# The first load moved ahead of the weight matrices on the loading queue

## The chip, the cores and the metric

The kernel runs on one core of a Trainium2 chip. The metric is the time of one execution in device microseconds; three runs of the kernel before took 325.69 to 325.96 us, median 325.85. A core has a matrix engine (TensorE, PE in the profile), a vector engine (VectorE, DVE), ScalarE (ACT), GpSimd (POOL) and SyncE (SP), each with a queue of its own, and 16 DMA engines that all of them share. Here ScalarE and SyncE compute nothing: ScalarE issues loads, SyncE issues stores.

## The reference

```python
# x: (128, 128, 1024) float32, itok_B_0_7: (128,) int32 in 0..7, L0_cond_weights: (8, 128, 128) float32
w = weights[subjects]                        # one 128 x 128 matrix for each of 128 samples
out = jnp.einsum('bct,bcd->bdt', x, w)       # B, C, D, T = 128, 128, 128, 1024
return x + out
```

Each sample is a matrix of 128 channels by 1024 times (512 KB). It is multiplied by the matrix of its subject, one of eight, and added to the product.

## The kernel before

The 128 samples are taken in 32 turns of four (`NT` = 32, index `i`), and each turn in two pairs (`j`, 64 pairs in all). Twelve buffers of four samples (`xs`, `SLOTS` = 12) hold what is loaded; a result is written back over its input, and stored from there. So a buffer goes from load to product, to addition, to store, and is loaded again twelve turns later.

All work is written out by hand, with semaphores. What each queue does, in its order:

- **ScalarE** issues the load of the eight weight matrices into `w_all` (line 161; 512 KB in 1024 pieces of 512 B, one row of one matrix each), and then the 128 loads of the samples (line 169, through `load` and `transfer`, where the profile has them as line 57). Each takes 512 KB in 32 pieces of 16 KB: the samples' rows are spread so that four rows of 4 KB lie together in memory. Until turn 12 nothing holds these loads back but the queue. From turn 12 on, ScalarE waits until the buffer has been stored (lines 164 to 167).
- **SyncE** issues the load of the 128 subject numbers (`given`, line 141), and then the stores (lines 221 to 223): two of 1 MB in turn 0, one of 2 MB in each turn from 1 to 30, and three pieces in turn 31.
- **VectorE** writes zeros (line 143), makes the subject numbers safe as indices (lines 153 to 157), and then adds product and input for one pair at a time (line 217).
- **GpSimd** reads indices into registers, 16 at a time (line 185), waits once for `w_all` (line 193), and copies the matrix of each sample out of `w_all` into one of four buffers (line 196). From the third pair on, the first copy of a pair also waits for the pair's loads, and for the addition two pairs ago.
- **TensorE** starts with three matmuls on zeros (line 146), waits for the loads of the first two pairs itself (line 181), and for the copies of a pair (line 203); then it multiplies, in pieces of 512 columns (line 206).

The two samples of a pair share one semaphore (`s_pair`), so a pair is free to go when both its samples have landed. At the end ScalarE waits for the last stores (lines 227 to 230).

What sets the order around the change is ScalarE's queue: its transfers go to the same 16 DMA engines one after the other, and in the trace the first packets of sample 0 start where the last ones of the matrices end. The stores come from another queue and mix with the loads.

Of the kernel before, what the change touches and what calls it, by code (L numbers as in the profile page):

```python
# [41 lines left out]
DMA = 16  # L42
# [7 lines left out]
def transfer(nc, engine, out, in_):  # L50

    later, nc._always_lower_symbolic_ap = nc._always_lower_symbolic_ap, False
    ins, outs = engine.lower_ap_dma(in_), engine.lower_ap_dma(out)
    nc._always_lower_symbolic_ap = later
    return engine.add_instruction(  # L57
        mybir.InstDMACopy(
            name=nc.get_next_instruction_name(),
            engine=engine.engine,  # L60
            ins=ins,
            outs=outs,
            mode="Copy",
            cce_op=ALU.bypass,
            queue=QUEUES[engine.engine],
        )
    )


@with_exitstack  # L70
def kernel(
    ctx: ExitStack,
    tc: tile.TileContext,
    x: bass.AP,
    subjects: bass.AP,
    weights: bass.AP,
    out: bass.AP,
):
    nc = tc.nc
    B, C, T = x.shape  # L80
    S, _, D = weights.shape
    NT = B // (G * H)

    def sbuf(name, *shape, dtype=F32):
        return ctx.enter_context(nc.sbuf_tensor(name, list(shape), dtype)).ap()

    given, near, wrap, index = (
        sbuf(name, 1, B, dtype=I32) for name in ("given", "near", "wrap", "index")
    )
    w_all = sbuf("w_all", C, S, D)  # L90
    ws = [sbuf(f"w{i}", C, 1, D) for i in range(W_SLOTS)]
    zeros = sbuf("zeros", C, N)
    xs = [sbuf(f"x{i}", C, H * G, T) for i in range(SLOTS)]
    ps = [
        ctx.enter_context(nc.psum_tensor(f"ps{i}", [D, G, T], F32)).ap() for i in range(P_SLOTS)
    ]

    s_given = tc.alloc_semaphore("s_given")
    s_wall = tc.alloc_semaphore("s_wall")
    s_index = tc.alloc_semaphore("s_index")  # L100
    s_zeros = tc.alloc_semaphore("s_zeros")
    s_copied = tc.alloc_semaphore("s_copied")
    s_product = tc.alloc_semaphore("s_product")
    s_added = tc.alloc_semaphore("s_added")

    s_pair = [[tc.alloc_semaphore(f"s_pair{i}_{h}") for h in range(H)] for i in range(SLOTS)]


    s_first = tc.alloc_semaphore("s_first")

    def emptied(i, h):

        turns = i // SLOTS
        return (DMA * G + (DMA if h == H - 1 else 0)) * turns

    def loaded(i, q):

        h = q // G
        return s_pair[i % SLOTS][h], emptied(i, h) + DMA * G

    def load(engine, i, q):
        k, h = i % SLOTS, q // G
        transfer(
            nc,
            engine,
            xs[k][:, q, :],
            x[i * H * G + q].rearrange("(a r) t -> a (r t)", r=ROWS),
        ).then_inc(s_pair[k][h], DMA)

    def store(i, q0, q1):  # L130
        k, b = i % SLOTS, i * H * G
        transfer(
            nc,
            nc.sync,
            out[b + q0 : b + q1].rearrange("g d t -> d g t"),
            xs[k][:, q0:q1, :].rearrange("d (o g) t -> d o (g t)", g=min(G, q1 - q0)),
        ).then_inc(s_first if i == 0 and q1 == G else s_pair[k][(q1 - 1) // G], DMA)

    with tc.tile_critical():  # L139

        nc.sync.dma_start(given, subjects.rearrange("(o b) -> o b", o=1)).then_inc(s_given, DMA)

        nc.vector.memset(zeros, 0.0).then_inc(s_zeros, 1)  # L143
        nc.tensor.wait_ge(s_zeros, 1)
        for _ in range(IDLE):
            nc.tensor.matmul(  # L146
                ps[P_SLOTS - 1][:, G - 1, :N], zeros[:, :D], zeros, start=True, stop=True
            )

        nc.vector.wait_ge(s_given, DMA)
        nc.vector.tensor_scalar(near, given, -S, S - 1, ALU.max, ALU.min).then_inc(s_index, 1)  # L153
        nc.vector.wait_ge(s_index, 1)
        nc.vector.tensor_scalar(wrap, near, 0, S, ALU.is_lt, ALU.mult).then_inc(s_index, 1)  # L155
        nc.vector.wait_ge(s_index, 2)
        nc.vector.tensor_tensor(index, near, wrap, ALU.add).then_inc(s_index, 1)  # L157
        nc.gpsimd.wait_ge(s_index, 3)


        nc.scalar.dma_start(w_all, weights.rearrange("s c d -> c s d")).then_inc(s_wall, DMA)  # L161
        for i in range(NT):
            k = i % SLOTS
            if i == SLOTS:
                nc.scalar.wait_ge(s_first, DMA)
            if i >= SLOTS:
                nc.scalar.wait_ge(s_pair[k][H - 1], emptied(i, H - 1))
            for q in range(H * G):
                load(nc.scalar, i, q)


        for j in range(NT * H):
            i, q0, q1 = j // H, j % H * G, (j % H + 1) * G
            k = i % SLOTS
            p = ps[j % P_SLOTS]

            ahead = j < P_SLOTS
            if ahead:  # L180
                nc.tensor.wait_ge(*loaded(i, q0))
            for q in range(q0, q1):
                b = i * H * G + q
                if b % R == 0:
                    _, subject = nc.values_load_multi_w_load_instructions(
                        index[0:1, b : b + R],
                        engines=[mybir.EngineType.Pool],
                        min_val=0,
                        max_val=S - 1,
                        skip_runtime_bounds_check_because="the index is clamped on the chip above",  # L190
                    )
                if b == 0:
                    nc.gpsimd.wait_ge(s_wall, DMA)
                if not ahead and q == q0:
                    nc.gpsimd.wait_ge(s_added, j - P_SLOTS + 1)
                copy = nc.gpsimd.tensor_copy(  # L196
                    ws[b % W_SLOTS], w_all[:, bass.ds(subject[b % R], 1), :]
                )
                if not ahead and q == q0:
                    copy.wait_op(*loaded(i, q0), "sem-ge")  # L200
            copy.then_inc(s_copied, 1)

            nc.tensor.wait_ge(s_copied, j + 1)
            for q in range(q0, q1):
                for t in range(0, T, N):
                    mm = nc.tensor.matmul(  # L206
                        p[:, q % G, t : t + N],
                        ws[(i * H * G + q) % W_SLOTS][:, 0, :],
                        xs[k][:, q, t : t + N],
                        start=True,  # L210
                        stop=True,
                    )
            mm.then_inc(s_product, 1)

            mine = xs[k][:, q0:q1, :]
            nc.vector.wait_ge(s_product, j + 1)
            nc.vector.tensor_tensor(  # L217
                mine, p, mine, ALU.add
            ).then_inc(s_added, 1)

            if i == 0 or q1 == H * G or i == NT - 1:
                nc.sync.wait_ge(s_added, j + 1)
                store(i, q0 if i in (0, NT - 1) else 0, q1 - (b == B - 1))

    with tc.tile_critical() as waits:
        for i in range(NT - SLOTS, NT):
            nc.scalar.wait_ge(s_pair[i % SLOTS][H - 1], emptied(i + SLOTS, H - 1))
        nc.scalar.wait_ge(s_pair[(NT - 1) % SLOTS][0], emptied(NT - 1 + SLOTS, 0) + DMA)  # L230
    last = nc.sync.dma_start(out[B - 1], xs[(NT - 1) % SLOTS][:, H * G - 1, :])

    tc.add_manual_dep(
        last.ins,
        waits.name,
        mybir.DependencyInfo(mybir.DependencyClass.NoSync, mybir.DependencyReason.SCHED_ONLY),
        reason="the end of the program waits for it",
    )
# [27 lines left out]
```

## Time and profile before

| | |
|---|---|
| median of three runs | 325.85 us (325.69 to 325.96) |
| the profiled execution | 326.15 us |
| its span, first to last instruction | 324.4 us |
| moved by DMA | 134.85 MB, 416 GB/s over the span |
| PE busy | 240.2 us (74%) |
| DVE busy | 147.9 us (46%) |
| POOL busy | 34.3 us (11%) |
| `w_all`, issue to landing | 4.3 us |
| a load of x, issue to landing (median) | 32.2 us |
| a store of 2 MB, issue to landing (median) | 46.9 us |

The profile is that of one execution. Its page divides the span into 40 slices of 8.1 us and gives for each the busy tenths of an engine and the rate of the DMA. Other views give a table for any stretch of time, the instructions in order of time, and, for a DMA, when it was issued and when it landed; the trace also has a record of each DMA packet, with its start, length, size and queue. The issue of a DMA is shown on the queue of its engine (ACTq, SPq); it is not counted as busy time, and the transfer itself starts later. A window counts a packet where it starts, so a share can be over 1 in a short stretch. The time of an execution is 1.77 us longer than the span in this profile; that part lies around the span.

### The profile page before, as it was taken

To read this page: it belongs to the slowest core of one execution; us is meant where nothing else is said; L and a number is where in the kernel's file an instruction comes from. 1 tells how busy PE (TensorE), PEld (TensorE's weight loads), DVE (VectorE), ACT (ScalarE), POOL (GpSimd) and SP (SyncE) were. 2 spreads that over 40 slices of the span, in tenths; PEclk is the share of its full clock that TensorE was granted. 3 is DMA by queue.
4 is the path that set the end of the run, shared out by engine and by line. 5 is a ranking of instruction groups with operands and counts; after the bars stand their busy time and mean duration, and the time that the engine had idled before them with its cause. 6 is when DMAs were issued, how large, how long until landed. Compare 5 with 4: busy or idle time off the path is not lost.

```text
span 324.4 us, 1608 instructions
## 1 busy us (share of the span) xinstructions
PE 240.2 (74%) x518; PEld 94.5 (29%) x518; DVE 147.9 (46%) x68; POOL 34.3 (11%) x132
## 2 busy tenths in 40 slices
PE   7999987888888888888988888888888768000000
PEld 2444432333333333333333333333333323000000
DVE  1475754555555555555555555554554553200000
POOL 1011110111111111111011111111111010000000
PEclk9999999999999999999999999999999999855555
DMA  7999999999999999999999999999999999999995
GB/s 263 402 418 426 426 421 425 425 425 423 428 425 422 427 418 427 427 424 424 428 423 421 423 427 426 419 429 426 423 426 427 417 435 417 425 427 424 429 426 243
DMA packets 16074, 134.85 MB, mean 416 GB/s; under 512 B 2625, under 2 KB 3650, under 8 KB 3906
## 3 DMA queue, kind: packets, MB, share of 16 engines
q10 hardware_dynamic: 7184, 67.64, 49.8%
q1 hardware_dynamic: 8882, 67.11, 49.3%
q8 instruction: 4, 0.07, 0.1%
q14 instruction: 4, 0.03, 0.0%
HBM read 67.63 MB, written 67.11 MB: 415 GB/s over the span
## 4 chain that ended last, share of the span: by engine, by line
PE 41%; DVE 20%; issue 18%; POOL 4%; DMA 2%; POOLq 1%; ACTq 0%; SPq 0%
PE ps L206 41%; DVE x L217 20%; POOL w L196 4%; DMA x<-in_x_dram 2%; POOLq L196 1%; ACTq L57 0%; ACTq L161 0%; ACTq L262 0%; SPq L139 0%
## 5 line engine op out<-in xcount | busy, mean ns | idle before, releaser
L206 PE MATMUL ps<-x,w 128*128 128x512 f32 x512 | 234.7, 604 | 33.6 <-POOL w L196 32.9
L217 DVE TENSOR_TENSOR x<-ps,x 128x2048 f32<-128x2048 f32 x64 | 146.7, 2292 | 128.1 <-PE ps L206 128.1
L206 PEld LDWEIGHTS ps<-x,w 128*128 128x128 f32 x512 | 92.6, 189 | 176.5 <-issue 92.3
L196 POOL COPY w<-w_all 128x128 f32 x128 | 34.1, 296 | 237.2 <-DMA x<-in_x_dram 207.2
L146 PE MATMUL ps<-zeros 128*128 128x512 f32 x6 | 5.5, 1088 | 1.7 <-DVE zeros L143 1.7
L146 PEld LDWEIGHTS ps<-zeros 128*128 128x128 f32 x6 | 1.8, 328 | 3.7 <-issue 2.1
L143 DVE MEMSET zeros<- 128x512 f32 x1 | 0.5, 485 | 1.1 <-SPq L139 1.1
L153 DVE TENSOR_SCALAR near<-given 1x128 int32<-1x128 int32 x1 | 0.2, 216 | 0.6 <-DMA given<-in_itok_B_dram 0.6
L157 DVE CUSTOM_DVE_ANT_0 index<-near,wrap 1x256 uint16<-1x256 uint16 x1 | 0.3, 278 | 0.0
L155 DVE TENSOR_SCALAR wrap<-near 1x128 int32<-1x128 int32 x1 | 0.2, 215 | 0.0
L253 POOL MEMSET const-float32-0.0<- 128x1 f32 x1 | 0.1, 99 | 0.2 <-issue 0.2
L253 POOL MEMSET const-bfloat16-1.0<- 128x1 bf16 x1 | 0.1, 102 | 0.0
L253 POOL MEMSET const-uint8-127<- 128x1 uint8 x1 | 0.1, 102 | 0.0
L253 POOL MEMSET const-float32-1.0<- 128x1 f32 x1 | 0.1, 99 | 0.0
## 6 DMA issues: line engine op xcount, KB each, us to landing
x<-in_x_dram ACTq DMA_DIRECT2D x128, 512.0 KB, 32.2
out_dram<-x SPq DMA_DIRECT2D x30, 2048.0 KB, 46.9
out_dram<-x SPq DMA_DIRECT2D x3, 1024.0 KB, 13.8
out_dram<-x SPq DMA_DIRECT2D x2, 512.0 KB, 21.0
w_all<-in_L_cond_weights_dram ACTq DMA_DIRECT2D x1, 512.0 KB, 4.3
given<-in_itok_B_dram SPq DMA_DIRECT2D x1, 0.5 KB
```

The source lines that it names most:

```text
L143: nc.vector.memset(zeros, 0.0).then_inc(s_zeros, 1)
L146: nc.tensor.matmul(ps[P_SLOTS - 1][:, G - 1, :N], zeros[:, :D], zeros, start=True, stop=True)
L153: nc.vector.tensor_scalar(near, given, -S, S - 1, ALU.max, ALU.min).then_inc(s_index, 1)
L155: nc.vector.tensor_scalar(wrap, near, 0, S, ALU.is_lt, ALU.mult).then_inc(s_index, 1)
L157: nc.vector.tensor_tensor(index, near, wrap, ALU.add).then_inc(s_index, 1)
L196: copy = nc.gpsimd.tensor_copy(ws[b % W_SLOTS], w_all[:, bass.ds(subject[b % R], 1), :])
L206: mm = nc.tensor.matmul(p[:, q % G, t : t + N], ws[(i * H * G + q) % W_SLOTS][:, 0, :], xs[k][:, q, t : t + N], start=True, stop=True,)
L217: nc.vector.tensor_tensor(mine, p, mine, ALU.add).then_inc(s_added, 1)
L253: nc = _bacc.Bacc("TRN2", target_bir_lowering=False, num_devices=1)
```

## The change

The load of the matrices is taken from its place ahead of the loop, and issued inside the loop behind the load of sample 0. The other 127 loads stay behind both. Nothing else is moved, and no wait is added or removed.

```diff
-        nc.scalar.dma_start(w_all, weights.rearrange("s c d -> c s d")).then_inc(s_wall, DMA)
         for i in range(NT):
             k = i % SLOTS
             if i == SLOTS:
...
             for q in range(H * G):
                 load(nc.scalar, i, q)
+                if i == 0 and q == 0:
+                    nc.scalar.dma_start(w_all, weights.rearrange("s c d -> c s d")).then_inc(s_wall, DMA)
```

## The prediction

> **What bounds the kernel now.** I read the 40 slices first, because the kernel moves 134.85 MB and computes little, then the DMA share stretch by stretch at both ends of the run, then the order of time around the first load. From the page:
>
> ```profile
> PE   7999987888888888888988888888888768000000
> DVE  1475754555555555555555555554554553200000
> ...
> DMA  7999999999999999999999999999999999999995
> GB/s 263 402 418 426 426 421 425 425 425 423 428 425 422 427 418 427 427 424 424 428 423 421 423 427 426 419 429 426 423 426 427 417 435 417 425 427 424 429 426 243
> ```
>
> The transfers are busy from the first slice to the last, at about 425 GB/s, while PE has nothing left for the last six slices. TensorE is high in the middle, but a data transfer ends the run 40 us after the last matmul. So the chain of waits, which gives 41% to PE, isn't the bound: a later matmul only means a later store in a queue that is full anyway. The time is: the moment the DMA engines start, plus the time their packets take, plus the gaps between packets, plus the uneven end. Windows over both ends (columns: stretch and length, busy time and count of PE, PEld, DVE, POOL, granted clock, DMA share, GB/s):
>
> ```profile
> 1.50:2.00 0.50, 0.32 (x1) 0.33 (x2) 0.12 (x1) 0.00 (x0) 1.00 0.00 1
> 2.00:2.50 0.50, 0.50 (x1) 0.17 (x1) 0.22 (x1) 0.00 (x0) 1.00 0.70 145
> 2.50:3.00 0.50, 0.50 (x2) 0.31 (x1) 0.47 (x2) 0.00 (x0) 1.00 0.29 60
> 3.00:3.50 0.50, 0.50 (x1) 0.03 (x1) 0.03 (x1) 0.00 (x0) 1.00 0.84 248
> 3.50:4.00 0.50, 0.50 (x2) 0.34 (x1) 0.00 (x0) 0.00 (x0) 1.00 0.98 291
> ```
>
> ```profile
> 5.50:6.75 1.25, 1.25 (x2) 0.09 (x1) 0.00 (x0) 0.91 (x4) 1.00 0.83 315
> 6.75:14.00 7.25, 6.55 (x16) 2.79 (x16) 2.29 (x1) 0.00 (x0) 1.00 1.02 416
> ...
> 24.00:272.00 248.00, 215.06 (x469) 84.11 (x468) 133.93 (x60) 31.50 (x118) 1.00 1.01 425
> 272.00:320.00 48.00, 3.50 (x8) 1.23 (x7) 3.78 (x2) 0.00 (x0) 0.59 1.01 426
> 320.00:323.00 3.00, 0.00 (x0) 0.00 (x0) 0.00 (x0) 0.00 (x0) 0.50 0.35 142
> ```
>
> From 24 to 320 us no DMA time is free. What an order of issue can still change lies ahead of 7 us: nothing flows until 2.04 us, the share is far under 1 while the matrices come in, and the rate dips once more from 5.5 to 6.75. The end (share 0.35) is the spread of the 16 engines, whose last packets end from 320.2 to 322.95 us in the packet records. Around the change, in order of time (start, length, engine, work):
>
> ```profile
> 0.93 0.43 ACTq L161 DMA_DIRECT2D w_all<-in_L_cond_weights_dram  x1
> 0.97 0.36 SPq L141 DMA_DIRECT2D given<-in_itok_B_dram  x1
> ...
> 1.39 12.87 ACTq L57 DMA_DIRECT2D x<-in_x_dram  x20
> ...
> 5.41 1.00 POOL L196 COPY w<-w_all 128x128 f32 x4 [4.96 <-DMA w_all<-in_L_cond_weights_dram]
> ...
> 7.86 6.71 PE L206 MATMUL ps<-x,w 128*128 128x512 f32 x15 [0.70 <-DMA x<-in_x_dram]
> ```
>
> **The change part by part.** Instruction counts stay; ScalarE's queue issues load 0, matrices, load 1, ... where it issued matrices, load 0, load 1, ... Load 0 takes 0.63 us to issue and the matrices 0.43 (0.46 with the pause between), so load 1 and all later loads are issued at the same 2.04 us as now.
>
> *The first byte.* The matrices' first packet starts at 2.04, 1.11 after their issue starts and 0.68 after it ends. No load of x is seen on an empty queue. If the delay counts from the start of the issue, load 0's first packet comes at 2.04, too; from the end, at 0.93 + 0.63 + 0.68 = 2.24. The subjects' little transfer (issued 0.97, packet at 1.90) is 0.93 from the start and 0.57 from the end, and decides nothing. A far row is the first store, issued at 13.92 with its first packet at 17.88, but behind a loading queue with over ten loads in it; at launch nothing is ahead, so I don't take it as a bound. I take 2.24, a cost of 0.20, with 0 as the other end.
>
> *The gaps.* From 2 to 4 us the shares miss 0.30, 0.71, 0.16 and 0.02 of half a microsecond each: 0.60 us of idle time on the mean engine. They are between packets: three packets alone took long (0.46 to 0.73 us); the other engines had none. After 3.3 us the matrices flow without gaps at about 297 GB/s (the 291 of the last row over its share), so their 524 kB need 1.77 us of full share. Now load 0 is waiting behind them, and can't fill the gaps. In the new order load 0 (524 kB at the 422 GB/s of 8 to 12 us: 1.24 us) runs from 2.24 to 3.48, and the matrices' descriptors, issued 0.65 later than now, are due from 2.69 on. By 3.48 they would have the first 0.79 us of the present ramp in store, some 92 kB (145 GB/s for 0.5 us, 60 for 0.33), enough for 0.31 us at 297 GB/s; the ramp needs 0.46 us more to reach full flow and itself brings 82 kB in that time. So no gap is left: worth 0.60, with 0 as the other end (it stays, wherever the matrices stand). The matrices then end at 3.48 + 1.77 = 5.25, where load 1 starts. In the packet records load 1's first packets now start at 5.34 to 6.03, by engine, mean 5.69. So the gain in DMA time is 5.69 - 5.25 = 0.44; counted by its parts it is 0.60 less 0.20, 0.40, and I take this.
>
> *The matrices' landing.* They land at 5.24 now, half a microsecond after their last packet; then at about 5.25 + 0.45 = 5.7. POOL stands at its wait for them, and behind it are the first four copies (1.00 us), of which two are needed for the first matmul: ready at 5.7 + 0.17 + 0.53 = 6.4. TensorE waits ahead of that for the first pair (samples 0 and 1), whose last part lands at 7.82, then about 7.4, and its idle matmuls last until 7.17. So 1.0 us of cover is left, and the later landing costs nothing. If that cover were gone, one pair of matmuls would be late, and the store that it feeds joins a loading queue that is full until about 270 us; nothing of that shows at the end.
>
> *Samples 0 and 1 earlier.* Load 0 lands over 2 us earlier, but the first wait is for the pair, and sample 1 comes 0.4 earlier only. The first store follows by as much. While loads run alone they move 416 GB/s, with stores among them 425: 0.4 us at 2% is under 0.01. SP's queue has only the subjects' transfer ahead of the stores; that starts at 1.90, before load 0's packets, and isn't delayed.
>
> *The dip of 5.5 to 6.75.* Six of load 1's first packets took 0.87 to 1.45 us instead of 0.62, five of them ending together at 6.8. At 315 instead of 416 GB/s it costs the mean engine 0.30 us, single ones up to 0.8. Nothing shows its cause, so I leave it where it is, at 0; if the new order removes it, the gain is 0.3 to 0.8; nothing speaks for a second one.
>
> **Sum.** The profiled execution took 326.15 us (span 324.4 and 1.77 around it), 0.30 over the median of 325.85. 326.15 + 0.20 - 0.60 = 325.75; off the median, 325.45. That is 0.12%, less than the 0.2% that a measurement of this kernel can tell from no change.
>
> **The rivals.**
>
> *The gaps belong to the start, not to the matrices* (first access to memory after launch). Then load 0 meets them, and only its longer issue remains: 325.85 + 0.20 = 326.05. For it: three slow packets at 2.27 to 2.36 look like slow first reads. Against: most engines had no packet in hand in the gap, and the matrices bring 64 packets per engine where a load brings two. [...]
>
> *The dip goes too.* 325.45 less 0.3 to 0.8: 324.65 to 325.15, say 325.05. For it: it strikes only the second load behind the matrices, 0.6 us after their last packet, and later loads at 416 GB/s have none. Against: it may belong to sample 1's place in memory, which is the same.
>
> *Slower: the matrices' descriptors aren't made while load 0 flows.* If they are taken up only when its packets are gone, the 0.68 of first delay and the whole present course (2.04 to 4.45, where load 0's packets start on the mean engine, 2.41 us) come after 3.48, and load 1 starts at 6.57, 0.88 later than now: 326.75. It is slower than can be told from no change from a start of load 1 beyond 6.3. For it: the first store's packets came 4 us after its issue, so one issue can stand behind others. Against: load 0 was issued at 1.39 to 2.01, while the matrices were flowing, and its packets follow theirs at a share of over 1 (4.0 to 4.5), without a gap.
>
> That the order does not change is excluded: the compiled ScalarE stream has load 0 ahead of the matrices.
>
> **How the numbers follow.** Gaps filled, 325.45: 0.43. Gaps stay, 326.05: 0.12. Dip goes too, 325.05: 0.30, since a stall that nothing explains is easily moved, and the last engine alone sets the end. Descriptors late, 326.75: 0.15. Under 325.2 is faster, over 326.5 slower: 0.30 faster, 0.55 same, 0.15 slower. The likeliest case alone has 325.25 to 325.65 (first byte at either end, gain 0.40 or 0.60, and 0.14 of spread between runs). The range leaves out the slow case and the far end of the dip's: 324.7 to 326.3.
>
> **What would show it.** In the new profile: first packets near 2.2 us at over 400 GB/s, then small packets at a share near 1 with no row like 0.29; load 1's packets from about 5.25; first matmul near 7.4; first store issued near 13.5; every window from 24 to 320 at 425 GB/s as now; and the last packet 0.4 earlier. I am wrong if a gap stands between load 0 and the matrices, if the dip is gone, or if the engines' spread at the end, 2.8 us now, is not the same: half a microsecond there is worth more than the whole change.

## The result and the profile after

The changed kernel takes 326.36 us (median of 21 runs, 325.85 to 327.31) against 325.84 us (21 runs, 325.48 to 326.85) of the kernel before: ratio 1.0017, 95% interval 1.0010 to 1.0024. It is 0.5 us slower. The prediction was 0.40 us faster; the measured time lies just above its range.

The profiled execution of the changed kernel took 326.14 us, in the lower third of its runs, and that of the kernel before 326.15, in the upper third of its own. So the two traces show how the head (the first microseconds of the traffic) changed; the difference in time has to come from the medians. From the page of the changed kernel, the granted clock, DMA share and rate in 40 slices:

```profile
PEclk9799999999999999999999999999999899655555
DMA  7999999999999999999999999999999999999996
GB/s 245 418 407 425 419 425 429 419 423 428 429 420 422 436 413 425 430 426 419 428 427 420 426 422 425 426 419 429 427 423 420 435 416 426 424 426 428 425 426 262
```

The picture is as before: the transfers fill the run. The second digit of the clock, 7, is new. The head of the changed kernel in windows (the columns are those of the prediction's windows):

```profile
2.00:2.50 0.50, 0.50 (x1) 0.18 (x1) 0.21 (x1) 0.00 (x0) 1.00 1.51 426
2.50:3.00 0.50, 0.50 (x2) 0.31 (x1) 0.46 (x2) 0.00 (x0) 1.00 0.32 98
3.00:3.50 0.50, 0.50 (x1) 0.03 (x1) 0.03 (x1) 0.00 (x0) 1.00 1.29 524
3.50:4.00 0.50, 0.50 (x2) 0.34 (x1) 0.00 (x0) 0.00 (x0) 1.00 0.18 36
...
5.50:6.00 0.50, 0.50 (x2) 0.00 (x0) 0.00 (x0) 0.00 (x0) 1.00 1.72 396
6.00:6.50 0.50, 0.15 (x1) 0.00 (x0) 0.00 (x0) 0.02 (x1) 1.00 0.55 229
6.50:7.00 0.50, 0.00 (x0) 0.00 (x0) 0.00 (x0) 0.50 (x3) 1.00 0.55 229
```

With packets of 16 KB these rows jump, because each counts a packet where it starts. Laid end to end by their records, packets fill the engines from 2.25 us on, nearly without a gap; but from 6 to 7 us, for one, the rows have 229 GB/s only, and some 280 if each packet's bytes are spread evenly over its length. That is the trap of this case: the engines are busy all the time, and slow. The other windows of the changed kernel:

```profile
5.50:6.75 1.25, 0.65 (x2) 0.00 (x0) 0.00 (x0) 0.27 (x2) 1.00 0.97 277
6.75:14.00 7.25, 5.66 (x9) 2.43 (x10) 0.22 (x1) 0.73 (x4) 0.76 1.00 411
...
24.00:272.00 248.00, 219.11 (x477) 86.72 (x476) 137.14 (x60) 31.23 (x118) 0.99 1.01 425
272.00:320.00 48.00, 2.04 (x5) 0.57 (x3) 2.65 (x2) 0.00 (x0) 0.56 1.01 425
320.00:323.00 3.00, 0.00 (x0) 0.00 (x0) 0.00 (x0) 0.00 (x0) 0.50 0.46 186
```

From 24 to 320 us nothing has changed: 425 GB/s at a share of 1.01 (426 at the end, before). The dip of 5.5 to 6.75 us is deeper, 277 instead of 315. In order of time around the change:

```profile
0.92 0.55 ACTq L57 DMA_DIRECT2D x<-in_x_dram  x1
...
1.50 0.59 ACTq L170 DMA_DIRECT2D w_all<-in_L_cond_weights_dram  x1
...
2.12 14.32 ACTq L57 DMA_DIRECT2D x<-in_x_dram  x22
...
6.48 0.99 POOL L197 COPY w<-w_all 128x128 f32 x4 [6.03 <-DMA w_all<-in_L_cond_weights_dram]
8.34 0.47 PEld L207 LDWEIGHTS ps<-x,w 128*128 128x128 f32 x2 [3.02 <-DMA x<-in_x_dram]
8.35 7.97 PE L207 MATMUL ps<-x,w 128*128 128x512 f32 x14 [2.19 <-DMA x<-in_x_dram]
```

The first matmul comes at 8.35 us instead of 7.86, and it waited for x, not for the copies. TensorE stood idle for 2.19 us ahead of it, and then ran its first matmuls at a granted clock of 0.57 (window of 8 to 12 us), one every 0.85 us instead of every 0.43; such a start is called cold below. The first store landed at 26.4 to 27.1 us instead of 24.2 to 25.0.

The page and its windows can't settle this, since they count packets where they start. Two measures worked out from the packet records make the heads comparable. The *excess* is the time by which the 16 KB packets of x took longer than 0.625 us, summed and divided by 16 engines, for packets that start before and after 3.9 us. The *lag* is the time less the bytes moved until then over 425.3 GB/s; two kernels can be compared in it at any time. The excess leaves out gaps between packets, and whatever slows the matrices' small ones; the lag has everything. The last column is the end of the last packet. The names are those of the experiments below.

```
                                 excess, us       lag, us, at        last
                             to 3.9  3.9 to 9     9      30        packet
kernel before                  0.00    0.26     3.51    3.90       322.96
changed kernel                 0.32    0.67     3.80    4.22       322.91
changed, once more             0.49    0.59     3.81    4.29       323.49
changed, five on zeros         0.45    0.37     3.68    4.23       323.66
changed, 2 ahead of 1          0.48    0.59     4.01    4.40       323.65
before, one on zeros           0.00    0.16     3.68    4.06       322.47
before, 1 ahead of 0           0.00    0.23     3.48    3.96       323.24
before, 1.6 us later           0.00    0.30     5.00    5.54       324.05
no matrices                    0.96    0.10     3.42    4.18       321.69
matrices on SyncE              0.29    0.10     3.25    3.69       322.36
matrices on SyncE, again       0.40    0.16     3.33    3.69       322.75
load 0 on SyncE                0.00    0.14     3.21    3.57       322.34
changed, load 1 on SyncE       0.33    0.13     3.35    3.87       322.54
before, large pieces           0.01    0.41     3.43    3.85       322.66
changed, large pieces          0.43    0.41     3.79    4.20       323.64
changed, behind load 1         0.38    0.32     3.95    4.42       323.15
changed, behind load 3         0.36    1.10     3.91    4.83       323.91
```

The lag that the head leaves stays: at 320 us it is 4.31 to 4.57 in the four traces of the changed order (second row to fifth) and 4.03 to 4.20 in three of the old (first, sixth and seventh row), 0.30 more on the mean, as much as at 30 us.

### The profile page after: what moved, and what is told of

Same layout as the page of the kernel before. It is cut to its first block, busy times and chain, and to the rows that moved or that the text cites. A ratio compares the mean times of both kernels' runs of the same rounds, so it can differ in the third digit from the quotient of the medians.

```text
span 324.3 us, 1608 instructions
## 1 busy us (share of the span) xinstructions
PE 241.3 (74%) x518; PEld 95.9 (30%) x518; DVE 147.9 (46%) x68; POOL 34.0 (10%) x132
## 4 chain that ended last, share of the span: by engine, by line
PE 44%; DVE 19%; issue 15%; POOL 4%; DMA 2%; POOLq 1%; ACTq 0%; SPq 0%
PE ps L207 44%; DVE x L218 19%; POOL w L197 4%; DMA x<-in_x_dram 2%; POOLq L197 1%; ACTq L170 0%; ACTq L57 0%; ACTq L263 0%; SPq L139 0%
## 5 line engine op out<-in xcount | busy, mean ns | idle before, releaser
L207 PEld LDWEIGHTS ps<-x,w 128*128 128x128 f32 x512 | 94.2, 192 | 173.7 <-issue 94.9
L146 PE MATMUL ps<-zeros 128*128 128x512 f32 x6 | 4.5, 904 | 1.7 <-DVE zeros L143 1.7
```

The costliest lines, as they stand in the source:

```text
L146: nc.tensor.matmul(ps[P_SLOTS - 1][:, G - 1, :N], zeros[:, :D], zeros, start=True, stop=True)
L207: mm = nc.tensor.matmul(p[:, q % G, t : t + N], ws[(i * H * G + q) % W_SLOTS][:, 0, :], xs[k][:, q, t : t + N], start=True, stop=True,)
```

## The experiments

Every time below is a median beside that of the kernel before in the same comparison.

**Is it the loads, or the cold TensorE?** The changed kernel once more (no edit), and two kernels that change only the matmuls on zeros:

> The changed kernel once more, beside the next three. Theory A (the head): load 1's first packets, which follow the matrices, take 0.7 to 1.75 us instead of 0.62, all samples behind them are 0.25 to 0.3 us late, and this shows at the end: 0.3 to 0.6 us slower than before. Theory B (the cold TensorE): TensorE stood idle from 6.15 to 8.35 us, ran its first matmuls at half clock (granted clock 0.57 from 8 to 12 us), the first store was about 2 us late, and that is what costs: also 0.3 to 0.6 us, but only in executions where the granted clock drops before 12 us.

```diff
 # changed kernel
-IDLE = 3
+IDLE = 5
```

> The changed kernel with five matmuls on zeros instead of three, so that TensorE is busy to 8 us or beyond and its first real matmuls run warm. Theory A (the head): no gain, within 0.15 us of the changed kernel, since the loads are as late as they were. Theory B (the cold TensorE): 0.3 to 0.6 us faster than the changed kernel, that is, level with the kernel before.

```diff
 # kernel before
-IDLE = 3
+IDLE = 1
```

> The kernel before with one matmul on zeros instead of three, so that TensorE is idle from about 4 to 8 us, the first real matmuls run at half clock, and the first store comes some 2 us later, with the loads as they were. Theory A (the head): within 0.15 us of before; at most 0.08, from 2 us more of loads alone, at 410 instead of 425 GB/s. Theory B (the cold TensorE): 0.3 to 0.6 us slower than before.

Measured beside 325.87 us: the changed kernel 326.52 (ratio 1.0019, 1.0010 to 1.0028), with five matmuls on zeros 326.60 (1.0019, 1.0010 to 1.0027), the kernel before with one 325.95 (1.0001, 0.9992 to 1.0010). The third has the cold start in full, in its windows,

```profile
5.00:8.00 3.00, 0.00 (x0) 0.00 (x0) 0.00 (x0) 1.00 (x4) 1.00 0.93 377
8.00:12.00 4.00, 3.44 (x4) 1.51 (x5) 0.00 (x0) 0.00 (x0) 1.00 0.97 401
```

four matmuls from 8 to 12 us, where the kernel before has ten, and its first store landed at 27.0 to 27.5 us. It costs nothing that can be measured. (In this trace the column of the granted clock stays at 1.00, although these matmuls take 0.86 us on the mean, so that column is no sure sign.) In the changed kernel with five matmuls TensorE idled for 0.44 us only, and it is as slow. The changed kernel once more didn't start cold at all in its trace, nine matmuls from 8 to 12 us, and that execution took 326.69. The cold TensorE is out.

**What is a microsecond at the head worth at the end?**

```diff
 # kernel before
+        nc.scalar.wait_ge(s_index, 1)
         nc.scalar.dma_start(w_all, weights.rearrange("s c d -> c s d")).then_inc(s_wall, DMA)
```

> The kernel before, with ScalarE made to wait ahead of the matrices until VectorE's first operation on the subject numbers has ended (2.47 us), so that every load is issued some 1.6 us later. It measures what a microsecond at the head is worth at the end. If the end follows the head one to one: 1.4 to 1.8 us slower. If the mixed stretch takes some of it up: under 1.2. What belongs to a fixed time after the launch stays at 5.3 to 6.8 us in the trace; what belongs to the order of the transfers moves by 1.6.

The matrices were issued at 2.50 us instead of 0.93, 1.57 later, and the kernel took 327.55 against 325.91 us, 1.64 more (ratio 1.0050, 1.0037 to 1.0063). The head counts one to one. Its slow packets moved along, from 5.3 to 6.9 us, so they belong to no fixed time.

**Whose are the slow packets?** First sample 1's place in memory, in both orders:

```diff
 # kernel before
-            for q in range(H * G):
+            for q in (1, 0, 2, 3) if i == 0 else range(H * G):
 # changed kernel, in another run
-            for q in range(H * G):
+            for q in (0, 2, 1, 3) if i == 0 else range(H * G):
```

> The kernel before with sample 1 loaded ahead of sample 0 (matrices, 1, 0, 2, 3). What the slow packets after the matrices belong to: if to sample 1's place in memory, they now follow the matrices' last packets directly, from about 4.2 us, and sample 0 behind has none; if to the second transfer behind the matrices, or to the time of 5.3 to 6.8 us, sample 0's packets now have them and sample 1's take 0.61 us. In time all theories give 325.85 within 0.3.

> The changed kernel with sample 2 loaded ahead of sample 1 (0, matrices, 2, 1, 3). If the slow packets belong to sample 1's place in memory, sample 2's take 0.61 us directly behind the matrices and sample 1's 0.7 to 1.6 after them. If to what comes third, sample 2's have them. The time is 326.5 us by either.

The swap in the kernel before took 325.95 against 325.87 us (1.0001, 0.9992 to 1.0009); single packets of both samples were slow, up to 0.98 us of sample 1's and 1.02 of sample 0's, so it settled nothing. In the changed order sample 2 had them: eight of its first packets took 1.46 to 1.62 us. It took 326.32 against 325.95 (1.0013, 1.0004 to 1.0022), as expected. Sample 1's place is out. Then the small pieces, in both orders:

```diff
-nc.scalar.dma_start(w_all, weights.rearrange("s c d -> c s d"))
+nc.scalar.dma_start(w_all, weights.rearrange("s (a e) d -> (s a) e d", e=8))
```

> The kernel before with the matrices loaded in 128 pieces of 4 KB (16 rows of one matrix to each 16 partitions; so the rows stand in the wrong place, and the products are those of mixed matrices) instead of 1024 of 512 B. If the gaps of 2 to 3.3 us are the small pieces' own, they go, and so does their overhead (1.77 us of share against 1.24): load 0's packets start at 3.3 to 3.7 instead of 4.1 to 4.8, and the time is 0.7 to 1.1 us shorter than before. If the gaps belong to the start of the traffic, they stay: 0.5 us at most.

> The changed kernel with the same large pieces (and the same mixed matrices). If the small pieces make the load behind them slow, that load's first packets now take about 0.62 us, and this kernel is within 0.2 us of the kernel before with large pieces: the order alone costs nothing. If the first transfers are slow whatever their pieces, load 1 stays slow, and it is 0.4 to 0.6 us slower than the kernel before with large pieces.

Before, with large pieces: 325.85 against 325.91 (0.9995, 0.9986 to 1.0004). Changed, with large pieces: 326.52 (1.0017, 1.0008 to 1.0026). So the small pieces cost nothing that shows at the end, and the order costs the same with large ones. The head of the kernel before says why, first as it is and then with large pieces:

```profile
2.00:3.50 1.50, 1.50 (x2) 0.51 (x2) 0.71 (x3) 0.00 (x0) 1.00 0.61 151
3.50:5.00 1.50, 1.50 (x3) 0.67 (x2) 0.00 (x0) 0.00 (x0) 1.00 1.23 439
5.00:8.00 3.00, 2.30 (x4) 0.48 (x3) 0.00 (x0) 1.00 (x4) 1.00 0.98 377
```

```profile
2.00:3.50 1.50, 1.50 (x2) 0.51 (x2) 0.71 (x3) 0.00 (x0) 1.00 0.69 229
3.50:5.00 1.50, 1.50 (x3) 0.67 (x2) 0.00 (x0) 0.16 (x1) 1.00 1.16 472
5.00:8.00 3.00, 1.21 (x3) 0.19 (x1) 0.00 (x0) 0.84 (x4) 1.00 0.95 350
```

The gap at the start stays (0.69; it was 0.61 with small pieces), and what is won by 5 us is lost from 5 to 8: 350 GB/s instead of 377. The gap is not the small pieces' own. Nor are the slow packets behind it: with large pieces both orders have the same excess after 3.9 us, 0.41, in packets strewn from 5 to 8 us, and the two differ in load 0's start alone (0.43 against 0.01).

Then the matrices' place, and the matrices themselves:

```diff
 # changed kernel
-                if i == 0 and q == 0:
+                if i == 0 and q == 1:
 # and, in another run
+                if i == 0 and q == 3:
```

> The changed kernel with the matrices behind load 1 instead of load 0 (0, 1, matrices, 2, ...). If the slow first packets belong to the load that follows the matrices, load 2's are now 0.7 to 1.6 us, load 1's take 0.61, and the time is as in the changed kernel, 0.4 to 0.6 us over before. If they belong to sample 1's place in memory, load 1 has them, directly behind load 0 at about 3.5 us, and load 2 none. If neither has them, the time is 0.3 to 0.5 us better than the changed kernel's, level with before.

> The changed kernel with the matrices behind load 3. The time has been 325.9, 326.5 and 327.1 us with none, one and two loads ahead of the matrices. If it grows with the place of the matrices, 327.5 to 328.5; if what costs is the slow stretch of 5 to 8 us alone, and not the matrices' place, 326.5 or less, since the matrices now come at about 7 us, and TensorE's later start (about 10 us) cost at most 0.1 in the kernel with one matmul on zeros.

Behind load 1: 327.10 against 325.91 us (1.0032, 1.0020 to 1.0044). Behind load 3: 326.76 against 325.95 (1.0023, 1.0012 to 1.0033). So it doesn't grow with the place, but the second isn't down at 326.5 either. (The trace of the first is of an execution of 326.36 us, one of its fastest, and doesn't show what made its median the highest.) My expectation that load 2 would be slow in the first of them was wrong: load 1 had seven packets of 0.8 to 1.75 us from 3.9 us on, and the matrices behind it came with gaps, as this window of 5.5 to 6.75 us shows:

```profile
5.50:6.75 1.25, 1.25 (x2) 0.08 (x1) 0.00 (x0) 0.00 (x0) 1.00 0.77 224
```

In the second, eleven of the sixteen first packets of load 2 took 1.6 to 1.9 us, from 5.2 us on; load 2 is the third transfer there, and the matrices come fifth, after 8 us. So the slowest stretch stands at what comes third, some 3 us after the first packet, ahead of the matrices as well as behind them. The bound isn't sharp: in both kernels some packets of load 1, the second transfer, were slow too.

```diff
 # kernel before; VectorE sets w_all to zero instead, and GpSimd waits for that (lines not shown)
-        nc.scalar.dma_start(w_all, weights.rearrange("s c d -> c s d")).then_inc(s_wall, DMA)
```

> The kernel before without the load of the matrices (VectorE sets w_all to zero, so the output is x): loads 0, 1, 2, ... alone. Theory C (the first reads after the launch are slow, whatever they are, and a second slow stretch comes some 3.3 us after the first packet, about the third transfer): load 0's first packets take 0.8 to 1.3 us as in the changed kernel, load 2's or a later load's are slow too, and the time falls by the matrices' bytes alone, 1.2 us (324.6). Theory D (the matrices make what follows them slow): no slow packets behind load 0, and the time falls by 1.5 to 2.

324.88 against 325.95 us (0.9971, 0.9961 to 0.9981): 1.07 less, where the bytes alone are worth 1.23. Without any matrices the first packets of load 0 took 1.27 to 1.93 us, and the head begins so:

```profile
2.00:3.50 1.50, 1.50 (x2) 0.51 (x2) 1.25 (x4) 0.00 (x0) 1.00 1.04 175
3.50:5.00 1.50, 1.50 (x3) 0.67 (x2) 0.00 (x0) 0.18 (x1) 1.00 0.86 350
5.00:8.00 3.00, 3.00 (x7) 1.13 (x6) 0.00 (x0) 0.82 (x4) 1.00 1.05 437
```

A slow start is there whatever comes first, but neither of one form nor of one size: in this kernel an excess of 0.96 us in one piece, and then no second slow stretch (437 GB/s from 5 to 8); with the matrices behind load 0, 0.32 to 0.49 and then the second stretch. In both, the excess up to 9 us comes to 0.8 to 1.1 in all. Theory C was right that load 0 is slow, though it had 0.8 to 1.3 us, and nearly right on the time, and wrong on the second stretch. Theory D was right that there is no second stretch, and wrong on the time.

**Two queues.** Now SyncE issues one of the first three transfers; the engines still carry load 0, the matrices and load 1. The queue isn't all that differs: some transfers are issued earlier, and their order on the engines can change.

```diff
 # kernel before
-        nc.scalar.dma_start(w_all, weights.rearrange("s c d -> c s d")).then_inc(s_wall, DMA)
+        nc.sync.dma_start(w_all, weights.rearrange("s c d -> c s d")).then_inc(s_wall, DMA)
```

> The matrices issued by SyncE behind the subject numbers, all loads by ScalarE, load 0 first: matrices and load 0 share the start. Theory C: the slow start is a stretch of time, and what waits in it overlaps, so nothing is lost against before: within 0.3 us of it. Theory D: load 0 and load 1 are both mixed with the matrices and both slow: 0.4 to 0.8 us slower than before, as the changed kernel.

> The matrices on SyncE's queue once more: 0.1 to 0.5 us under before by both theories, if the first measurement holds.

```diff
 # changed kernel
-                load(nc.scalar, i, q)
+                load(nc.sync if i == 0 and q == 1 else nc.scalar, i, q)
```

> The changed kernel with load 1 issued by SyncE, behind the subject numbers; ScalarE issues load 0, matrices, load 2, ... Theory E (a large load behind the matrices on the same queue starts slowly): load 2's first packets take 0.7 to 1.6 us, load 1's do not, and the time is 0.2 to 0.6 us over before. Theory F (the start of the traffic is slow for about a microsecond per engine in all, and two queues at work from the start shorten it): no slow stretch after 5 us, and the time is that of before or up to 0.4 less, as with the matrices on SyncE's queue.

```diff
 # kernel before
-                load(nc.scalar, i, q)
+                load(nc.sync if i == 0 and q == 0 else nc.scalar, i, q)
```

> The kernel before with load 0 issued by SyncE behind the subject numbers; ScalarE issues matrices, load 1, ... Load 0 can fill the gap of 2.4 to 3.2 us in the matrices' stream from its own queue. Theory E: load 1 behind the matrices is slow as in the changed kernel, no gain: 325.9 to 326.4. Theory F: the gap is filled and nothing is paid back, 0.2 to 0.5 us under before.

Matrices on SyncE: 325.65 against 325.95 us (0.9989, 0.9980 to 0.9998), and again 325.84 against 325.90 (0.9996, 0.9987 to 1.0005), less than expected. Load 1 on SyncE: 325.84 against 325.90 (0.9997, 0.9987 to 1.0006). Load 0 on SyncE: 325.77 (0.9995, 0.9986 to 1.0004), between what the two theories gave; it didn't fill the gap, since its own first packets came at 4.0 us only. The stretch from 5.5 us, in the changed kernel first and then with the matrices on SyncE:

```profile
5.50:6.75 1.25, 0.65 (x2) 0.00 (x0) 0.00 (x0) 0.27 (x2) 1.00 0.97 277
6.75:8.00 1.25, 0.00 (x0) 0.00 (x0) 0.00 (x0) 0.73 (x4) 1.00 1.07 419
```

```profile
5.50:6.75 1.25, 1.08 (x2) 0.09 (x1) 0.00 (x0) 0.00 (x0) 1.00 1.08 426
6.75:8.00 1.25, 0.01 (x1) 0.01 (x1) 0.00 (x0) 1.00 (x4) 1.00 1.02 419
```

426 GB/s instead of 277: the second slow stretch is gone, though load 1 follows load 0 and the matrices in the same order and at the same time (its first packets start at 5.29 to 6.0 us; 5.22 to 5.8 in the changed kernel). It was issued earlier, though, at 1.48 instead of 2.12 us, and no run tells whether that matters. Load 1 on SyncE differs from the changed kernel in one transfer's queue, and its excess after 3.9 us falls from between 0.37 and 0.67 (four traces) to 0.13, its time by some 0.6 us. But there load 1 comes second, from 3.85 us on, and the matrices third, from 4.5 to 7.6. That is the order of the run with the matrices behind load 1, which on one queue took 327.10 us and had a lag of 3.95 at 9 us, against 3.35 here. Load 2, which there follows the matrices on ScalarE's queue, takes 0.61 to 0.73 us, so theory E falls. As versions to use, these three are at best 0.06 to 0.3 us better than the kernel before, and only one of four intervals excludes no change.

## Why the prediction was wrong

By its own steps:

- *The first byte:* predicted 2.24, measured 2.25 us. That is partly luck: load 0 took 0.55 us to issue instead of 0.63, and its first packet came 0.78 us after that instead of 0.68.
- *The gaps, worth 0.60:* that they go in the new order was right, and that they were the matrices' own was wrong. The matrices flowed without a gap and took 1.77 us per engine, as predicted, but load 0 had met the slow start instead: its first packets took 0.80 to 1.1 us (mean 0.92) instead of 0.61, an excess of 0.32. What showed as gaps between small packets seems to show as length of large ones. The rival "the gaps belong to the start", with 326.05, had the right mechanism here, as the kernel without matrices shows, where load 0 is slow with no matrices about. That gaps and length are one and the same loss isn't shown; their sizes differ (0.60 in gaps, an excess of 0.32 to 0.96). The Trainium skill, "DMA: Bandwidth & Descriptors", section "Anatomy of one DMA — SWDGE (gpsimd) path", calls descriptor generation small, but for transfers that GpSimd issues; these come from ScalarE, so the page doesn't settle it. The kernel with large pieces speaks against gaps of the small pieces' own, since its share at the start stays at 0.69.
- *The dip, left at 0:* this is the other step that failed. It grew from an excess of 0.26 to 0.67 in the two profiled executions (0.37 to 0.59 in the other traces of the changed order, 0.16 and 0.23 in those of the old). In the changed kernel all sixteen first packets of load 1 were slow, 0.69 to 1.75 us; before, six. That it would go was given a chance of 0.30; of a second one it says that nothing speaks for it.
- *The sum:* predicted -0.40. With 0.32 for load 0 and 0.41 for the dip it becomes +0.33. The lag at 9 us went from 3.51 to 3.80, +0.29. So the sum closes in the head.
- *The matrices' descriptors:* the rival that they come late, 326.75, did not happen, although 326.36 lies between its time and that of the rival above. The matrices' first packets start at 3.67 us, while load 0's last are under way until 4.26.
- *The matrices' landing and TensorE:* the matrices landed at 6.32 us instead of the 5.7 predicted; the cover held, since the first matmul waited for x. It came at 8.35 instead of 7.4, and cold. That this is free, as the prediction said of a late matmul, was shown by the kernel with one matmul on zeros.
- *One to one to the end:* right, 1.64 us for 1.57 in the kernel with the delay.
- *The end:* of the 0.5 us, the head explains about 0.3. In four traces of the changed order the lag at 30 us is 4.22 to 4.40, in three of the old order 3.90 to 4.06, 0.31 between the means; the last packet ends 0.54 later on the mean (323.43 against 322.89). The lag at 320 us still differs by 0.30, so the other 0.2 us lies in how far the last engine ends behind the others. The prediction named that spread as worth more than the change, and no run here tells what moves it.

What stays open is what the second slow stretch is. Shown: it is not sample 1, not the small pieces, not TensorE, not a fixed time after the launch; it begins some 3 us after the first packet, mostly at the third transfer, also ahead of the matrices; it is missing without the matrices, and where the first three transfers come from two queues. Whether the queue itself does it, or the earlier issue and other order that came with the second queue, was not separated.

## What to carry to other kernels

A gap at the start of the traffic need not be free time that another transfer can fill: try first whether it belongs to what stands there, by putting something else there. A full DMA share is no sign of full rate; read the GB/s beside it, and the length of a packet of known size. When the first transfers of a kernel are reordered, test them also on two queues, since here the order cost 0.5 to 0.6 us on one and nothing that could be measured on two.

## What was unexpected in the hardware

- The first large reads after the launch were slow where a load of x came first: a 16 KB packet took 0.80 to 1.1 us in the changed kernel and up to 1.93 without the matrices, against 0.61 later.
- Splitting the first three transfers over two issuing queues removed a slow stretch (277 to 426 GB/s from 5.5 to 6.75 us), though the same 16 DMA engines carry both; why is open.
- A matmul stream that starts cold, with the first store landing over 2 us late, cost nothing in this kernel: 325.95 against 325.87 us.
- Loads alone ran at 638 ns per 16 KB packet from 8 to 15 us in the kernel before, and at 617 from 24 to 272, with stores among them.
